# Moving steps between the turns of a fused attention and expert kernel

## The chip, the cores and the metric

One NeuronCore of a Trainium2 chip runs the whole computation. The metric is the device time of one execution in microseconds (us), for which a lower number is better. The kernel before takes 1458.46 us as the median of three runs (1452.64 to 1461.51). Beside these there is one profiled execution, from which every duration below is read.

## The reference

The input `x` has 8 batches of 512 tokens of 256 numbers, all float32. First comes attention with a convolution in the middle of it; then a second attention with a mixture of experts.

```python
# layer 1, on layernorm(x); 16 heads of 16, causal
q, k, v = split(x @ Wqkv.T + b)
ctx = attention(q, k, v)
q2  = conv1d(ctx, conv_w, width 3, padding 1) + conv_b    # over the tokens
x   = x + attention(q2, k, v) @ out_w.T + out_b
# layer 2, on layernorm(x)
h   = x + attention(rope(rmsnorm(x) @ wq), rope(rmsnorm(x) @ wk), rmsnorm(x) @ wv) @ wo
xf  = rmsnorm(h)
probs = softmax(xf @ w_router); the two largest of 8, scaled to a sum of 1
y   = h + sum over experts e of combine[e] * ((silu(xf @ wg[e]) * (xf @ wu[e])) @ wd[e])
```

In layer 2, `x` in the first line and in the sum `h` is that layer's normed input, as in the code; the outer residual is added to the whole. Every batch thus needs three attentions, and every token two of eight experts of width 704.

## The kernel before, in words

**Pairs and turns.** The batches go in four pairs, of which one batch is lane 0 (`one` in the plan) and the other lane 1 (`two`). Six attentions of a pair follow each other: `attention1` of lane 0 and of lane 1, `attention2` of both, `attention3` of both. An attention is a generator of nine steps. A step multiplies queries and keys into scores in PSUM (L1212, TensorE), takes the exponential of 1,024 columns twice (L1219, ScalarE) and masks the diagonal blocks (L1227, GpSimd). Its value products (L1142, TensorE) are not issued at once: they are put in the list `behind` and issued later by `catch_up`. A **turn** is two steps, so a pair takes 27 turns, and 108 turns make up the first 60% of the span.

**What else a turn holds.** The order on TensorE, VectorE, ScalarE and GpSimd is written out by hand: an engine executes what the program issues for it in that order. Between the steps stands all the other work of the pair, as units that the table of `plan` calls gives to a turn: `plan(t + 4, before1, "transpose3", 1)` means that in the fifth turn of this pair the method `transpose3(1)` of the previous pair's lane 1 is called. `before0` and `before1` are the batches of the pair before, `one` and `two` those of this pair, `next0` and `next1` those of the pair after. Units in `units` are called at the end of the turn, those in `first_units` and `small_units` between its two steps. Some work is delayed further: `follow(n, f, where)` calls `f` n turns later at "mid" (between the steps), "late" (after the second step, ahead of the turn's units) or "end" (after the units).

**The units that matter here.**
- `stats` and `normed` (L1305, L1320) are the first layer norm, on VectorE with a power on GpSimd (L1315); `transpose` (L1292, TensorE) turns the result, and VectorE or ScalarE copies it out of PSUM (L1296). `fetch_next` loads a batch from SP's queue.
- `q`, `k` and `values` are the projections (L1052, L1070 on TensorE). They are read out of PSUM at L1359 (VectorE) or L1357 (ScalarE), at L1342 (ScalarE) and at L1088 (VectorE, into the tile `va`).
- `normalise` (L1152) ends half an attention: ScalarE copies the sums (L1159), SP moves rows (L1167, L1168), and `finish` on VectorE takes reciprocals and products (L1172, L1173). In `attention1` the step `differences` follows (L1396 to L1399, the tiles `terms`), from which `conv` multiplies its quarters (L1408) and combines them (L1417 on ScalarE; L1422, L1426 on VectorE).
- `k2` and `q2` project and rotate (L1502 to L1508), and `values2` (L1534) projects the values of the third attention; its parameter `soon` decides whether VectorE or ScalarE copies into `va` (L1084).
- `h` (L1541) is the output projection: TensorE (L1041), an addition on VectorE (L1547), one on GpSimd (L1548), and squares on ScalarE that are written back into the same PSUM bank (L1550). `rms` (L1555) stores the batch and scales its rows (L1557, L1558, L1561).
- `transpose3` (L1565) turns the rows; the copy out of PSUM is VectorE's (L1298) with `soon` and ScalarE's (L1302) without. `logits` (L1568), `route` (L1583; some 25 tiny VectorE operations and one exponential, L1597) and `slots` (L1616; two small products, L1626 and L1627, and 16 tiny VectorE operations) choose the experts. Then GpSimd sends the rows to their places in DRAM, one transfer a step (L1650).

**Banks.** All units share two PSUM banks (`mm_tile`, L991), which they take in turn: a unit's product waits until the last but one has been read. The scores have two tiles of their own.

**Experts.** After the turns come 24 tiles of 384 tokens (`expert_tile`, L734). The first of them begins in the last turns: a generator whose first part turns the rows (L742, L745), whose second fetches sums, and whose next six are the hidden products (L764) with their activation (L778).

Of the kernel before, what the change touches and what calls it, by code (L numbers as in the profile page):

```python
# [19 lines left out]
B, S, D = 8, 512, 256  # L20
# [603 lines left out]
def fast_path(  # L624
# [29 lines left out]
    TURNS = 3 * STEPS  # L654
# [193 lines left out]
    with ExitStack() as att:  # L848
# [266 lines left out]
        def follow(turns, f, where):  # L1115
            due[where].append([turns, f])
# [6 lines left out]

        masked = []

        def attention(qT, kT, v, to, then=None, soon=False):

# [22 lines left out]
            def normalise(ch):  # L1152


                k = next(n_sums)
                cs = [big.tile([P, S], F32, tag=f"cs{i}", name=f"cs{i}") for i in range(2)]
                r = big.tile([P, S], F32, tag="r", name="r")
                for i in range(2):
                    nc.scalar.activation(  # L1159
                        cs[i], av[i], AF.Copy, accum_out=total[:, i, k : k + 1]  # L1160
                    )

                def part(t, i):
                    return t.rearrange("(f i) n -> i f n", i=2)[i]

                for i in range(2):
                    nc.sync.dma_start(part(r, i), part(cs[i], 1 - i))  # L1167
                nc.sync.dma_start(part(cs[1], 0), part(cs[0], 0))  # L1168

                def finish(n0):  # L1170
                    half = slice(n0, n0 + S // 2)
                    nc.vector.reciprocal(r[:, half], r[:, half])  # L1172
                    nc.vector.tensor_tensor(to[:, ch, half], cs[1][:, half], r[:, half], ALU.mult)  # L1173

                def check():
                    nc.scalar.activation(cs[0], r, AF.Copy, accum_out=rtotal[:, k : k + 1])

                where = ("mid", "late" if soon else "end")[ch]
                for n0 in range(0, S, S // 2):
                    follow(1 - ch, lambda n0=n0: finish(n0), where)  # L1180
                if then is not None:
                    follow(1 - ch, lambda: then(ch), where)
                follow(3 - 2 * ch, check, "late")
# [5 lines left out]
            mid = NB // 2  # L1189
# [65 lines left out]
        class Batch:  # L1255
# [108 lines left out]
            def attention1(self):  # L1364

                cx = self.cx = self.context_tile("cx")
                nc.gpsimd.memset(cx[:, :, 0:1], 0.0)
                nc.gpsimd.memset(cx[:, :, S + 1 : S + 2], 0.0)
                self.terms = {}
                return attention(  # L1370
                    self.qT, self.kT, self.v, cx[:, :, 1 : S + 1], self.differences, self.lane == 0
                )

# [295 lines left out]
        batches = [Batch(b) for b in range(B)]  # L1671
        units = collections.defaultdict(list)
# [3 lines left out]
        busy = set()  # L1676
# [5 lines left out]
        def plan(turn, t, what, *several, among=units):  # L1682
            if t is not None:
                if among is units and what not in NO_MATMULS:
                    busy.add(turn)
                for args in several or [()]:
                    args = args if isinstance(args, tuple) else (args,)
                    among[turn].append(unit(t, what, *args))
# [4 lines left out]
        for p in range(B // 2 + 1):  # L1693

            before0, before1, one, two, next0, next1 = (batch(2 * p + i) for i in range(-2, 4))
            if one is None:
                next0 = next1 = None
            t = p * TURNS
            plan(t, before0, "transpose3", (0, True), (1, True))
            plan(t, two, "q", 0)  # L1700
            plan(t, before0, "logits")
            plan(t + 1, two, "values", 0)
            plan(t + 1, before0, "route")
            plan(t + 1, before1, "normed2", 2, 3)
            plan(t + 1, next0, "stats")
            plan(t + 2, before1, "h", 0, 1)
            plan(t + 2, before0, "slots")
            plan(t + 2, before1, "rms")
            plan(t + 3, two, "q", 1, among=first_units)
            plan(t + 3, two, "k", 1)  # L1710
            plan(t + 3, next0, "fetch_next")
            plan(t + 3, next0, "normed")
            plan(t + 4, before1, "transpose3", (0, True))
            plan(t + 4, two, "values", 1)
            plan(t + 4, before1, "transpose3", 1)
            plan(t + 5, next0, "transpose", (0, True), (1, True), among=first_units)
            plan(t + 5, next0, "q", (0, True))
            plan(t + 6, before1, "logits")
            plan(t + 6, one, "conv", (0, 0))
            plan(t + 7, before1, "route")  # L1720
            plan(t + 7, one, "conv", (0, 1), (1, 0))
            plan(t + 8, one, "conv", (1, 1))
            plan(t + 9, next0, "k", 0)
            plan(t + 10, next0, "values", 0)
            plan(t + 10, before1, "slots")
            plan(t + 11, next0, "values", 1)
            for c in range(NC):
                plan(t + 10 + c, one, "bias", c)
                plan(t + 14 + c, two, "bias", c)
            plan(t + 12, two, "conv", (0, 0), among=first_units)  # L1730
            plan(t + 12, two, "conv", (0, 1))
            plan(t + 13, next0, "k", 1)
            plan(t + 14, two, "conv", (1, 0), among=first_units)
            plan(t + 14, two, "conv", (1, 1))
            plan(t + 15, one, "x1", 0, 1)
            plan(t + 16, next0, "q", 1)
            plan(t + 16, one, "transpose2", 0, 1)
            plan(t + 16, one, "k2", 0)
            plan(t + 16, one, "q2", 0)
            plan(t + 17, one, "q2", 1)  # L1740
            plan(t + 17, one, "k2", 1)
            plan(t + 18, one, "values2", 0, 1)
            plan(t + 19, two, "x1", 0, among=first_units)
            plan(t + 19, two, "x1", 1)
            plan(t + 20, one, "normed2", 0, 1, among=small_units)
            plan(t + 20, two, "transpose2", 0, 1)
            plan(t + 20, two, "k2", 0)
            plan(t + 21, two, "q2", (0, True), among=first_units)
            plan(t + 21, two, "k2", 1)
            plan(t + 20, next1, "stats")  # L1750
            plan(t + 21, next1, "fetch_next")
            plan(t + 21, next1, "normed")
            plan(t + 22, one, "normed2", 2, 3, among=small_units)
            plan(t + 23, two, "values2", (1, True), among=first_units)
            if next1 is not None:
                plan(t + 22, two, "q2", (1, False, False))
                plan(t + 23, two, "values2", (0, True))
                plan(t + 24, one, "h", 0)
                plan(t + 24, next1, "transpose", (0, True), (1, True))
                plan(t + 25, one, "h", 1)  # L1760
                plan(t + 25, one, "rms")
                plan(t + 26, two, "normed2", 0, 1, among=small_units)
                plan(t + 26, next1, "k", 0)
            else:
                plan(t + 22, two, "values2", 0)
                plan(t + 22, two, "q2", (1, False, False))
                plan(t + 24, one, "h", 0, 1)
                plan(t + 24, one, "rms")
                plan(t + 25, one, "transpose3", 0, 1)
                plan(t + 25, two, "normed2", 0, 1)  # L1770
                plan(t + 26, two, "normed2", 2, 3, among=small_units)
                plan(t + 26, one, "logits")
                plan(t + 26, one, "route")


        n_turns = B // 2 * TURNS
# [7 lines left out]
        one, two, later = batches[:3]  # L1784
# [32 lines left out]
        with tc.manual_schedule(  # L1817
# [3 lines left out]

            for _ in range(2):
                ps = mm_tile()
                for i in range(12):
                    nc.tensor.transpose(ps[:, i % NC * P : (i % NC + 1) * P], ident, ident)
            one, two = batches[:2]
            one.stats()
# [55 lines left out]
            first = {}  # L1883
# [4 lines left out]
                first["tile"] = expert_tile(first["weights"], rows, room)  # L1888

            units[n_turns - 4].append(first_tile_starts)  # L1890
            for n, parts_of in ((n_turns - 1, 4),):
                for _ in range(parts_of):
                    units[n].append(lambda: next(first["tile"]))
            steps = all_steps()
            for n in range(n_turns):
                behind_this = next(steps)

                rest = None if n in busy else max(1, len(behind) - 1)

                if n % TURNS in (6, 15, 24) and n in busy:  # L1900
                    rest = 2
                catch_up(rest)
                before_this = len(behind)
# [29 lines left out]
            t = batches[B - 1]  # L1933
# [103 lines left out]
```

## Time and profile before

| | |
|---|---|
| median of three runs | 1458.46 us (1452.64 to 1461.51) |
| the profiled execution | 1454.27 us |
| its span, first to last instruction | 1452.3 us |
| TensorE busy (products / weight loads) | 1384.3 / 893.9 us |
| VectorE, ScalarE, GpSimd busy | 744.0, 719.3, 580.2 us |
| mean granted TensorE clock | 0.985 |
| score and value products (L1212, L1142), busy | 282.9 and 224.0 us |
| expert products (L764, L788), busy | 347.0 and 190.9 us |
| first score exponential of turn 0, of turn 107 | 20.0 and 867.5 us |

How to read it: a busy TensorE need not be at its peak, since ends of products are modelled, but its idle time is read directly. A wait is put down to the instruction that came last. A granted clock below 1 means that products ran slower in that stretch.

### The profile page before, as it was taken

Reading aid. Unit: us, or ns where it says so; the run is one execution under the profiler, and the core shown is the slowest. Engines: PE = TensorE matmul, PEld = TensorE weight load, DVE = VectorE, ACT = ScalarE, POOL = GpSimd, SP = SyncE. Lnnn points to the kernel's source line nnn. Section 1 sums busy time; section 2 is a strip of 40 time slices with the busy share of each in tenths; the row PEclk is TensorE's granted clock in tenths of the full one; section 3 lists DMA queues with packets and bytes.
Section 4 is the critical chain, followed back from the end, with each engine's and each line's share of the span. In section 5 each row is a group of like instructions: output and inputs, shape, how many; then the busy total and the mean of one; then the engine's idle time right before and its main releaser. Section 6 shows DMA issues by size and latency. Waiting matters only on the chain. (4 is left out here: it accounts for less than half of the span.)

```text
span 1452.3 us, 32154 instructions
## 1 busy us (share of the span) xinstructions
PE 1384.3 (95%) x13466; PEld 893.9 (62%) x13466; DVE 744.0 (51%) x1467; ACT 719.3 (50%) x1164; POOL 580.2 (40%) x621
## 2 busy tenths in 40 slices
PE   8999989899989899989999998999999999999995
PEld 5566555566555566555565565666767667677673
DVE  4745886765886775885666865322222222222221
ACT  4677767577777676767676782311111111111110
POOL 3334333536433546433646345433233332332322
PEclk9999999999999999999999999999999999999998
DMA  5122122201001201011212022323131323232200
GB/s 147 58 80 87 63 78 75 75 31 61 16 24 52 93 31 57 16 43 38 88 58 81 24 78 83 113 83 117 42 110 47 105 64 98 60 107 86 84 20 16
DMA packets 62841, 97.61 MB, mean 67 GB/s; under 512 B 13516, under 2 KB 39064, under 8 KB 62688
## 3 DMA queue, kind: packets, MB, share of 16 engines
q1 hardware_dynamic: 52608, 69.74, 14.9%
q0 software_dynamic: 10080, 25.74, 5.3%
q8 instruction: 107, 1.75, 0.5%
q14 instruction: 46, 0.38, 0.1%
HBM read 46.06 MB, written 32.61 MB: 54 GB/s over the span
## 5 line engine op out<-in xcount | busy, mean ns | idle before, releaser
L1219 ACT ACTIVATE pr<-sc 128x1024 f32<-128x1024 f32 x432 | 418.8, 1023 | 169.2 <-PE sc L1212 168.2
L1227 POOL TENSOR_TENSOR pr<-pr,seen 128x512 f32<-128x512 f32 (+1 forms) x216 | 257.1, 1191 | 415.4 <-ACT pr L1219 407.1
L764 PE MATMUL pgu<-xgT,gu 128*128 128x384 f32 x1056 | 347.0, 488 | 1.6 <-DVE hT L779 1.6
L764 PEld LDWEIGHTS pgu<-xgT,gu 128*128 128x128 f32 x1056 | 200.7, 191 | 137.1 <-DVE hT L779 2.2
L778 ACT ACTIVATE sg<-pgu 128x384 f32<-128x384 f32 x120 | 58.8, 490 | 414.7 <-PE pgu L764 414.7
L1142 PE MATMUL av<-pr,va 64*32 64x448 f32 (+7 forms) x6144 | 224.0, 416 | 5.3 <-DVE va L1084 5.3
L779 DVE TENSOR_TENSOR hT<-sg,pgu 128x384 f32<-128x384 f32 x120 | 66.4, 554 | 247.0 <-ACT sg L778 247.0
L788 PE MATMUL po<-dn,hT 128*128 128x256 f32 x864 | 190.9, 379 | 1.6 <-POOL hT L759 1.6
L1212 PE MATMUL sc<-qT,kT 32*128 32x512 f32 (+7 forms) x2048 | 189.3, 440 | 2.9 <-ACT pr L1219 2.7
L805 POOL DMA_INDIRECT out_dram<-so_far,xg x72 | 72.4, 1006 | 288.8 <-DVE so_far L795 220.7
L1142 PEld LDWEIGHTS av<-pr,va 64*32 64x32 f32 x6144 | 113.7, 108 | 113.7 <-issue 84.4
L1172 DVE RECIPROCAL r<-r 128x256 f32<-128x256 f32 x96 | 167.5, 1745 | 27.2 <-DMA r<-cs 27.0
L788 PEld LDWEIGHTS po<-dn,hT 128*128 128x128 f32 x864 | 162.4, 190 | 23.6 <-POOL hT L759 2.0
L1212 PEld LDWEIGHTS sc<-qT,kT 32*128 32x128 f32 x2048 | 114.8, 186 | 75.6 <-issue 29.3
L795 DVE SCALAR_TENSOR_TENSOR so_far<-po,xg,so_far 128x256 f32<-128x256 f32 x72 | 34.8, 484 | 150.1 <-PE po L788 150.1
L750 POOL DMA_INDIRECT so_far<-out_dram,xg x72 | 74.0, 1028 | 53.7 <-issue 51.9
L1212 PE MATMUL sc<-q2T,kT 32*128 32x64 f32 (+7 forms) x1024 | 93.6, 434 | 0.8 <-ACT pr L1219 0.6
L1650 POOL DMA_INDIRECT xtab<-rows,slot x64 | 65.0, 1016 | 39.6 <-DVE pick L1639 23.5
L1212 PEld LDWEIGHTS sc<-q2T,kT 32*128 32x128 f32 x1024 | 58.1, 184 | 32.7 <-issue 14.6
L1408 PE MATMUL mm<-terms,conv_sb 128*128 128x256 f32 x256 | 63.5, 391 | 3.7 <-DVE terms L1397 3.7
L1052 PE MATMUL mm<-xT,wqkv_sb 128*128 128x512 f32 x128 | 64.3, 630 | 1.5 <-DVE xmT L1298 1.2
L1052 PE MATMUL mm<-xaT,wqkv_sb 128*128 128x512 f32 x128 | 61.3, 612 | 2.0 <-DVE xaT L1298 2.0
(178 smaller groups left out, 1355.3 us busy)
## 6 DMA issues: line engine op xcount, KB each, us to landing
r<-cs SPq DMA_DIRECT2D x96, 128.0 KB, 2.0
xtab<-pad SPq DMA_DIRECT2D x24, 397.5 KB, 3.5
xg<-xtab SPq DMA_DIRECT2D x24, 397.5 KB, 3.1
gu<-in_wg_dram SPq DMA_DIRECT2D x18, 352.0 KB, 3.2
cs<-cs SPq DMA_DIRECT2D x48, 128.0 KB, 1.9
dn<-in_wd_dram SPq DMA_DIRECT2D x9, 640.0 KB, 4.7
gu<-in_wu_dram SPq DMA_DIRECT2D x18, 320.0 KB, 4.3
out_dram<-x SPq DMA_DIRECT2D x9, 512.0 KB, 3.0
```

What stands on the lines that cost most here:

```text
L750: nc.gpsimd.indirect_dma_start(out=so_far[:, s, :], out_offset=None, in_=out, in_offset=token_of(xg, s), bounds_check=B * S - 1, oob_is_er ...
L764: nc.tensor.matmul(ps, gu[d][:, n0 : n0 + P], xgT[:, d, :], start=(d == 0), stop=(d == DC - 1),)
L779: nc.vector.tensor_mul(hT[k], sg, pu)
L788: nc.tensor.matmul(po, hT[k][:, s * P : (s + 1) * P], dn[:, k, :], start=(k == 0), stop=(k == NK - 1),)
L805: nc.gpsimd.indirect_dma_start(out=out, out_offset=token_of(xg, s), in_=so_far[:, s, :], in_offset=None, bounds_check=B * S - 1, oob_is_er ...
L1052: nc.tensor.matmul(ps, w[:, d, n0 : n0 + P], srcT[:, d, :S], start=(d == 0), stop=(d == DC - 1),)
L1142: nc.tensor.matmul(av[i][g * HP : (g + 1) * HP, j * KB :], v[rows, j, ch * G + g, :], pr[rows, g, at : at + n], start=(j == 0), stop=(j == ...
L1172: nc.vector.reciprocal(r[:, half], r[:, half])
L1212: nc.tensor.matmul(sc[:, g - g0, at : at + S - j * KB], kT[r0 : r0 + HP, ch, j], qT[r0 : r0 + HP, ch, j * KB : S], start=True, stop=True,)
L1219: nc.scalar.activation(pr[:, g0 : g0 + 2], sc, AF.Exp, scale=SCALE)
L1227: nc.gpsimd.tensor_tensor(diag, diag, seen.unsqueeze(1).unsqueeze(1).to_broadcast([P, G, len(parts), KB]), ALU.mult,).ins
L1650: nc.gpsimd.indirect_dma_start(out=xtab, out_offset=bass.IndirectOffsetOnAxis(ap=slot[:, c, k : k + 1], axis=0), in_=rows[:, c, :], in_off ...
```

## The change

The units are moved, and some copies out of PSUM change their engine:
- `attention` loses the parameter `soon`. In `attention1` of lane 0 the second `finish` and `differences` came at "late"; they now come at "end".
- `values2(0)` of lane 1 at t+23 and `transpose3(0)` of the previous lane 1 at t+4 lose their `True`, so ScalarE copies in place of VectorE.
- `next1.transpose` goes from t+24 to t+25.
- `next0.stats` goes from t+1 to t, and `slots` goes ahead of `h` in t+2.
- The quarters of lane 0's `conv` go from t+6, t+7 (two) and t+8 to t+7 (two, ahead of `route`), t+8 and t+9. `next0.values(0)` goes from t+10 to t+6, and `next0.k(0)` from t+9 to t+10.
- In the last pair `route` goes from the head of the last turn's expert work to a place behind three parts of the first expert tile.
- The number of transposes of the identity at the start, whose results nobody reads, goes from 2 × 12 to 2 × 17.
- In the last turns `catch_up` is no longer held to two entries (turn 96 is the one concerned).

```diff
...
         masked = []
-        def attention(qT, kT, v, to, then=None, soon=False):
+        def attention(qT, kT, v, to, then=None):
...
                 def check():
                     nc.scalar.activation(cs[0], r, AF.Copy, accum_out=rtotal[:, k : k + 1])
-                where = ("mid", "late" if soon else "end")[ch]
+                where = ("mid", "end")[ch]
                 for n0 in range(0, S, S // 2):
                     follow(1 - ch, lambda n0=n0: finish(n0), where)
                 if then is not None:
...
                 nc.gpsimd.memset(cx[:, :, 0:1], 0.0)
                 nc.gpsimd.memset(cx[:, :, S + 1 : S + 2], 0.0)
                 self.terms = {}
-                return attention(
-                    self.qT, self.kT, self.v, cx[:, :, 1 : S + 1], self.differences, self.lane == 0
-                )
+                return attention(self.qT, self.kT, self.v, cx[:, :, 1 : S + 1], self.differences)
...
             plan(t, before0, "transpose3", (0, True), (1, True))
             plan(t, two, "q", 0)
             plan(t, before0, "logits")
+            plan(t, next0, "stats")
             plan(t + 1, two, "values", 0)
             plan(t + 1, before0, "route")
             plan(t + 1, before1, "normed2", 2, 3)
-            plan(t + 1, next0, "stats")
+            plan(t + 2, before0, "slots")
             plan(t + 2, before1, "h", 0, 1)
-            plan(t + 2, before0, "slots")
             plan(t + 2, before1, "rms")
             plan(t + 3, two, "q", 1, among=first_units)
             plan(t + 3, two, "k", 1)
             plan(t + 3, next0, "fetch_next")
             plan(t + 3, next0, "normed")
-            plan(t + 4, before1, "transpose3", (0, True))
+            plan(t + 4, before1, "transpose3", 0)
             plan(t + 4, two, "values", 1)
             plan(t + 4, before1, "transpose3", 1)
             plan(t + 5, next0, "transpose", (0, True), (1, True), among=first_units)
             plan(t + 5, next0, "q", (0, True))
             plan(t + 6, before1, "logits")
-            plan(t + 6, one, "conv", (0, 0))
+            plan(t + 6, next0, "values", 0)
+            plan(t + 7, one, "conv", (0, 0), (0, 1))
             plan(t + 7, before1, "route")
-            plan(t + 7, one, "conv", (0, 1), (1, 0))
-            plan(t + 8, one, "conv", (1, 1))
-            plan(t + 9, next0, "k", 0)
-            plan(t + 10, next0, "values", 0)
+            plan(t + 8, one, "conv", (1, 0))
+            plan(t + 9, one, "conv", (1, 1))
+            plan(t + 10, next0, "k", 0)
             plan(t + 10, before1, "slots")
             plan(t + 11, next0, "values", 1)
             for c in range(NC):
...
             plan(t + 23, two, "values2", (1, True), among=first_units)
             if next1 is not None:
                 plan(t + 22, two, "q2", (1, False, False))
-                plan(t + 23, two, "values2", (0, True))
+                plan(t + 23, two, "values2", 0)
                 plan(t + 24, one, "h", 0)
-                plan(t + 24, next1, "transpose", (0, True), (1, True))
+                plan(t + 25, next1, "transpose", (0, True), (1, True))
                 plan(t + 25, one, "h", 1)
                 plan(t + 25, one, "rms")
                 plan(t + 26, two, "normed2", 0, 1, among=small_units)
...
                 plan(t + 25, two, "normed2", 0, 1)
                 plan(t + 26, two, "normed2", 2, 3, among=small_units)
                 plan(t + 26, one, "logits")
-                plan(t + 26, one, "route")
         n_turns = B // 2 * TURNS
...
             for _ in range(2):
                 ps = mm_tile()
-                for i in range(12):
+                for i in range(17):
                     nc.tensor.transpose(ps[:, i % NC * P : (i % NC + 1) * P], ident, ident)
             one, two = batches[:2]
             one.stats()
...
                 first["tile"] = expert_tile(first["weights"], rows, room)
             units[n_turns - 4].append(first_tile_starts)
-            for n, parts_of in ((n_turns - 1, 4),):
-                for _ in range(parts_of):
-                    units[n].append(lambda: next(first["tile"]))
+            for part in range(4):
+                if part == 3:
+                    plan(n_turns - 1, batches[B - 2], "route")
+                units[n_turns - 1].append(lambda: next(first["tile"]))
             steps = all_steps()
             for n in range(n_turns):
                 behind_this = next(steps)
                 rest = None if n in busy else max(1, len(behind) - 1)
-                if n % TURNS in (6, 15, 24) and n in busy:
+                if n % TURNS in (6, 15, 24) and n in busy and n + TURNS // 2 < n_turns:
                     rest = 2
                 catch_up(rest)
                 before_this = len(behind)
```

## The prediction

> **What bounds the kernel now.** First the page: TensorE (PE) is busy for 95% of the span, no other engine for more than 51%, and all of them wait for one another through TensorE's products. What can be won is therefore the time in which TensorE stands still, 1452.3 − 1384.3 = 68 us, and the time in which its clock is halved: a mean clock of 0.985 over the span is 22 us of lost clock, of which some 7 us lie behind the last product. The shares of busy time:
>
> ```profile
> PE 1384.3 (95%) x13466; PEld 893.9 (62%) x13466; DVE 744.0 (51%) x1467; ACT 719.3 (50%) x1164; POOL 580.2 (40%) x621
> ```
>
> Next, for whom TensorE waits (total, times, longest, in us). The first four lines and the sixth are results in PSUM that VectorE (DVE) or ScalarE (ACT) has not yet read, or tiles that they have not yet written:
>
> ```profile
> PE mm L1292 <- DVE xmT L1298: 8.6, 2, 4.4
> PE mm L1292 <- ACT mm L1550: 5.6, 3, 1.9
> PE av L1142 <- DVE va L1084: 5.3, 3, 1.8
> PE mm L1408 <- DVE terms L1397: 3.7, 4, 2.7
> ...
> PE mm L1587 <- DVE t L1581: 3.0, 1, 3.0
> ...
> PE mm L1626 <- ACT mm L1550: 1.8, 2, 1.1
> ```
>
> Third, the clock around two of them, by stretch (length, busy time of PE, PEld, DVE, ACT, POOL, then PEclk). In the stretch with the wait TensorE is busy for about half; in the next it is granted half the clock:
>
> ```profile
> 202.70:206.10 3.40, 1.78 (x26) 1.20 (x20) 3.33 (x4) 2.35 (x3) 1.42 (x1) 1.00 0.20 68
> 206.10:209.60 3.50, 3.34 (x40) 1.61 (x44) 3.35 (x5) 1.40 (x3) 1.28 (x1) 0.51 0.29 89
> 271.00:274.40 3.40, 0.72 (x14) 0.47 (x10) 3.24 (x6) 0.26 (x1) 1.84 (x2) 1.00 0.11 40
> 274.40:281.20 6.80, 5.24 (x53) 2.82 (x54) 2.79 (x6) 2.63 (x4) 0.00 (x0) 0.50 0.01 2
> ```
>
> So a wait of 1.8 us can cost 3.5. Last, why VectorE is late, in its timeline. Before the read of `va` it works off a rotation (L1505 to L1508):
>
> ```profile
> 203.76 1.64 DVE L1508 TENSOR_TENSOR qT<-t,t 128x512 f32<-128x512 f32 x1
> 205.43 1.41 DVE L1084 COPY va<-mm 64x512 f32<-64x512 f32 x2
> 206.87 1.75 DVE L1172 RECIPROCAL r<-r 128x256 f32<-128x256 f32 x1
> ```
>
> **What the skill says.** The Trainium skill, "TensorE: Matmul & The Clock Gate", section "What's actually happening", has the clock halved by an idle window of 3413 ns and restored by a busy one, with windows that run on freely. The trace agrees: its half-clock stretches are 3.4 or 6.8 us, and the same 1.78 us wait at 425.3, across a boundary, halves nothing. "PSUM — Partial Sum Buffer", "Engine vs sequencer instructions": ScalarE's and VectorE's queues are strictly first in, first out; so a moved step delays all behind it, as above. "SBUF — State Buffer", "Who interferes with whom": some VectorE operations wait for GpSimd's use of a shared port. The trace has L1561 at 335 to 2305 ns for one shape. "ScalarE: Activation LUTs", "What ACT_TABLE_LOAD costs": 1283 ns for a load and 1380 more for a drain; the trace shows loads of 1283 ns.
>
> **The change part by part.** All against the profiled execution's 1454.3 us (span 1452.3 and 2.0 around it). t is a pair's first turn.
>
> *Idle products.* 24 take 5.38 us and end at 8.05; the first real transposes wait until 9.79, and the clock is halved from 11.6 to 15.0. Ten more at 0.224 end at 10.3, at the 0.136 of a full-clock transpose (8 in 1.09) at 9.4: a cost of 0 to 0.5. If the half-clock stretch goes, 1.7 is won. I take −1.5 (−1.7 to +0.5).
>
> *`values2(0)` by ScalarE at t+23; the next batch's transposes at t+25 instead of t+24 (three pairs).* Each pair loses 1.78 (L1142 for `va`) and 1.88 (the second transpose at L1292, whose PSUM bank ScalarE squares into at L1550). The product ends at 203.16, ScalarE's exponentials at 203.29; two copies at 0.63 end near 204.6, and TensorE arrives at 204.49: 0.1 to 0.2 remain. The exponentials behind the copies start 0.3 late, with a score tile to spare. VectorE is freed of 1.4, so the first half of `c` stands at 205.4 + 1.75 + 0.43 = 207.6, and `h(0)` comes at 207.7, just behind it. One turn later the transposes' copies fall into an idle VectorE (3.2 busy of 10 us); `h(1)` needs the first one's bank, 0.2. At t+25 ScalarE's checks, squares and exponentials follow closely: 0.2. Won: 3 × (3.66 − 0.6) = 9.2. The half-clock stretches at 206, 216, 643 and 653 give 4 × 1.7 = 6.8, so −16.0 (−18 to −6).
>
> *`transpose3(0)` by ScalarE at t+4 (pairs 1 and 2; in pair 3 nothing waited).* VectorE reaches its copy only at 275.16, behind two reciprocals and four `terms`. ScalarE is free at 271.3, copies in 0.70, and TensorE, done at 271.72, waits 0.3. Won: 4.24 + 4.40 − 0.6 = 8.0. The half-clock stretches are 6.8 (5.24 busy, 2.6 lost) and 3.4 (1.7): 4.3. What is late next is VectorE's `va` (L1088) in the bank that the transposes of `xn` need. It would end at 276.6 and TensorE arrive at 275; the reciprocals start about 1 us sooner, since `rows` (L1561) no longer stand behind `slots`. I take no wait and keep 1.7 in the range: −12.3 (−14 to −8).
>
> *`stats` at t, `slots` before `h` at t+2.* `stats` puts 2.3 us on VectorE ahead of two reciprocals, so the `route` behind them comes 0.9 late; ScalarE's `prob` (L1597) is 0.9 late, and with it the exponentials behind it: TensorE's wait at 249.8 (0.81) grows to 1.7. `slots` takes 16 tiny products first. Their 4.0 us on VectorE (8 at 0.2, then 0.34, 1.11 and six at 0.2) now precede L1547, on which squares, exponentials and the next `q(1)` wait in turn. Worked through: L1547 at 257.1 (was 254.4), squares end at 259.8, exponentials start there (was 258.1), and `k(1)` starts at 262.3 (was 261.5). Two waits at L1626 (0.74, 1.08) are gone in that figure. Pair 3 had no such wait and loses 1.0. Queues passed: GpSimd's power (L1315) and the store that `rms` issues on SP move by about a microsecond, the load behind that store too; the row transfers still go out after the turn. +0.8 +0.8 +1.0, and 0.8 for a chance of a half-clock stretch: +3.4 (−1 to +8).
>
> *Convolution at t+7 to t+9, values at t+6, keys at t+10.* The wait for `terms` goes: 0.72 in pair 0, 0.15 in pair 1. `conv(0,0)`, `conv(0,1)` and `route` share two banks, and `route` then waits about 0.35 for L1422 in pairs 1 and 2. In pair 3 (2.69) nothing fills the turn, and ScalarE's exponentials and checks leave a new wait of 1.1 to 1.5 at L1212. Keys still follow the last quarter, whose `terms` lie in their tile. Sum −1.6 (−3.5 to +2).
>
> *`route` after three parts of the first expert tile.* The wait of 2.97 for L1581 stays in another dress: the second transposed half takes the bank of `logits`, which L1581 reads at 874.2. From 871.75 that is 2.4; the products start 0.9 earlier. Two more table loads fall between two activations, where ScalarE waits 2.1 us for products; uncovered they are 2 × 1.28, with the page's drain 2 × 2.66 as an estimate. −1.0 (−2.7 to +4).
>
> *`soon` and `rest`.* Between "late" and "end" of that turn stands no VectorE instruction, so the order there is the same: 0. One value product moves by half a turn in pair 3: 0 (±0.5).
>
> Sum: −1.5 − 16.0 − 12.3 + 3.4 − 1.6 − 1.0 = −29.0, so 1454.3 − 29.0 = 1425.3. The median shown is 4.2 above the profiled execution: 1429.5, rounded to **1430**.
>
> **Rivals.** *The next consumer waits instead* (0.13): `h(0)` has 0.1 us to spare behind `c`, and L1508 shows 1.64 where a free port gives 0.69. At 2 us in three turns, and 1.7 with a half-clock stretch of 1.7 in two, 12.8 come back: 1442. For it: VectorE is busy without a break from 262 to 277. Against: it idles 4.6 us right after.
> *The half-clock stretches stay* (0.10): windows run freely, and waits of 1.7 (turn 29) and 2.4 (first tile) remain. Seven stretches, 12 us: 1441.5. Against: a wait below 1.6 halved nothing.
> *Slower* (0.04): `stats` and `slots` on VectorE ahead of L1547 at t+2. If the shared port stretches them (L1637 took 1.11 instead of 0.19), L1547 is 6 us or more late, ScalarE holds the exponentials behind its squares, TensorE idles through whole windows in that turn and the two after it. It decides from 11 us per pair, when three outweigh the other steps' 32.4; at 6 us in each of three turns, 1454.3 − 32.4 + 54 + 4.2 = 1480.
>
> **The numbers.** This forecast 0.73, its own range 1419 to 1439. About 1% (14.6 us) is what a measurement of this kernel can tell from no change, so the bound is 1443.9. The two middle rivals lie below it with some six tenths of their chance: faster 0.86, same 0.11, slower 0.03. The range for 8 in 10 is 1418 to 1445: below, every step at its better end (−40.9, so 1417.6); above, both middle rivals in part.
>
> **What would show it.** Right: no `va L1084` by DVE, `xmT L1298` of 4 us or `mm L1550` among TensorE's waits; its idle time near 50 us; a clock of about 0.99. Wrong: waits at L1041 for `c`, at L1292 for `va L1088`, or at L1212 for exponentials in turns 29 and 30 (of 83 and 84 too) of more than 2 us, and half-clock stretches there.

## The result and the profile after

The kernel after takes **1441.05 us** (median of four executions, 1439.65 to 1443.23), the kernel before 1456.63 on the same chip (1452.64 to 1461.51). The ratio is 0.9893, with an interval of 0.9857 to 0.9928: 1.07% faster. The profiled execution of after takes 1439.65 us, its span is 1437.7 us and its mean clock 0.989. Profile against profile, after is 14.6 us shorter, where 29.0 were forecast.

TensorE stays as busy as it was (1384.3 and 1385.2 us, now with ten products more at the start); its gaps above 0.15 us went from 50.9 us to 35.1 us in all. So what was won is idle time. That the half-clock stretches up to the last product fell from 30.7 us to 17.1 in all did not make the busy time shorter; why is not shown. The first line below is the page's line of busy times, the others are TensorE's waits (total, times, longest, in us) from the view of waits of after. Its lines from about L1371 on are numbered two below those of before.

```profile
PE 1385.2 (96%) x13476; PEld 900.1 (63%) x13476; DVE 734.2 (51%) x1458; ACT 725.7 (50%) x1175; POOL 579.7 (40%) x621
...
PE sc L1212 <- ACT pr L1219: 7.1, 7, 2.3
PE mm L1292 <- DVE va L1088: 4.7, 2, 4.4
...
PE sc L1212 <- ACT kT L1519: 1.9, 3, 0.6
PE mm L1624 <- DVE both L1603: 1.7, 3, 0.9
...
PE mm L1041 <- DVE xT L1296: 1.0, 3, 0.3
```

The waits that the prediction set out to remove are gone: at L1292 for L1298 and for L1550, at L1142 for `va`, at L1408 for `terms`. New are three kinds: exponentials that come late (2.26 and 2.25 us in turns 29 and 56), the read of `va` (4.39 us), and small ones of 0.63 and 0.35 us behind `values2`. Two of the half-clock stretches of after, of 6.8 and 3.4 us, follow waits of the first two kinds (start and end, length, busy time of PE, PEld, DVE, ACT, POOL, PEclk, DMA share, GB/s):

```profile
242.40:245.80 3.40, 1.20 (x6) 0.59 (x8) 2.64 (x14) 3.02 (x5) 0.20 (x1) 1.00 0.02 5
245.80:252.60 6.80, 6.80 (x19) 4.43 (x17) 5.20 (x23) 2.05 (x2) 1.83 (x2) 0.50 0.00 0
484.70:488.10 3.40, 0.00 (x0) 0.00 (x0) 3.39 (x6) 1.27 (x5) 2.29 (x2) 1.00 0.26 97
488.10:491.60 3.50, 3.33 (x20) 2.50 (x24) 2.04 (x4) 0.00 (x0) 0.00 (x0) 0.51 0.15 57
```

From 484.7 to 488.1 TensorE does nothing at all, waiting for `va`. VectorE's timeline there (start, duration, operation, and in brackets how long it stood idle and for what) has the reason. SP's queue (the second view: start, duration, transfer) has the reason behind it:

```profile
471.95 2.51 DVE L1323 TENSOR_SCALAR xn<-x,mv,rstd 128x256 f32<-128x256 f32 x4
477.92 1.75 DVE L1172 RECIPROCAL r<-r 128x256 f32<-128x256 f32 x1 [3.46 <-DMA r<-cs]
481.73 0.43 DVE L1173 TENSOR_TENSOR cx<-cs,r 128x256 f32<-128x256 f32 x1 [2.05 <-DMA cs<-cs]
...
486.74 1.39 DVE L1088 TENSOR_TENSOR va<-mm,bv_sb 64x512 f32<-64x512 f32 x2
```
```profile
468.08 0.38 SPq L1266 DMA_DIRECT2D out_dram<-x  x1
471.10 0.38 SPq L679 DMA_DIRECT2D x<-in_x_dram  x1
471.58 1.11 SPq L1167 DMA_DIRECT2D r<-cs  x2
475.48 0.38 SPq L1266 DMA_DIRECT2D out_dram<-x  x1
477.91 0.47 SPq L1168 DMA_DIRECT2D cs<-cs  x1
```

VectorE is free at 474.5 and stands still for 3.46 us, because the rows for the reciprocal have not landed. They were issued at 471.58, behind the load of a batch that had itself waited for a store to land (468.08 to 471.10), and they arrive at 477.9, 6.3 us after their issue. The rows for `cx`, issued only then, cost another 2.05 us. The page of before gives 2.0 us as the median for one set of such rows. In before the same two sets took 6.0 us too (479.50 to 485.45, when L1168, which waits for them, goes out), but VectorE came to them only at 485.72, straight from the operation before, and waited for nothing:

```profile
479.50 1.11 SPq L1167 DMA_DIRECT2D r<-cs  x2
...
485.45 0.47 SPq L1168 DMA_DIRECT2D cs<-cs  x1
```
```profile
485.72 1.74 DVE L1172 RECIPROCAL r<-r 128x256 f32<-128x256 f32 x1
```

Where the 14.6 us came from is read from the start of each turn's first exponential, after minus before. A half-clock stretch counts in the turn that it falls in:

| stretch (turns) | forecast | profile |
|---|---|---|
| start to turn 0 (idle products) | −1.5 | −2.1 |
| `values2(0)` and transposes, three pairs (24–26, 51–53, 78–79) | −16.0 | −12.0 |
| `transpose3`, `stats`, `slots` (27–36, 53–64, 82–87) | −12.3 + 3.4 | +2.9 (−1.9, +2.4, +2.4) |
| the rest: convolution, drift, tail | −2.6 | −3.4 |

### The profile page after: what moved, and what is told of

Same layout as the page of the kernel before. It is cut to its first block, busy times and chain, and to the rows that moved or that the text cites. A ratio compares the mean times of both kernels' runs of the same rounds, so it can differ in the third digit from the quotient of the medians.

```text
span 1437.7 us, 32181 instructions
## 1 busy us (share of the span) xinstructions
PE 1385.2 (96%) x13476; PEld 900.1 (63%) x13476; DVE 734.2 (51%) x1458; ACT 725.7 (50%) x1175; POOL 579.7 (40%) x621
## 5 line engine op out<-in xcount | busy, mean ns | idle before, releaser
L1142 PE MATMUL av<-pr,va 64*32 64x512 f32 (+7 forms) x6144 | 218.9, 407 | 0.0
L1212 PE MATMUL sc<-qT,kT 32*128 32x320 f32 (+7 forms) x2048 | 192.4, 436 | 8.3 <-ACT pr L1219 6.2
L1172 DVE RECIPROCAL r<-r 128x256 f32<-128x256 f32 x96 | 167.5, 1744 | 20.5 <-DMA r<-cs 20.4
L1142 PEld LDWEIGHTS av<-pr,va 64*32 64x32 f32 x6144 | 113.4, 106 | 102.5 <-issue 73.7
L1212 PE MATMUL sc<-q2T,kT 32*128 32x512 f32 (+7 forms) x1024 | 95.0, 434 | 1.3 <-ACT pr L1219 0.9
L1648 POOL DMA_INDIRECT xtab<-rows,slot x64 | 64.6, 1009 | 32.1 <-DVE pick L1637 15.6
```

The source lines that it names most:

```text
L1142: nc.tensor.matmul(av[i][g * HP : (g + 1) * HP, j * KB :], v[rows, j, ch * G + g, :], pr[rows, g, at : at + n], start=(j == 0), stop=(j == ...
L1212: nc.tensor.matmul(sc[:, g - g0, at : at + S - j * KB], kT[r0 : r0 + HP, ch, j], qT[r0 : r0 + HP, ch, j * KB : S], start=True, stop=True,)
L1648: nc.gpsimd.indirect_dma_start(out=xtab, out_offset=bass.IndirectOffsetOnAxis(ap=slot[:, c, k : k + 1], axis=0), in_=rows[:, c, :], in_off ...
```

## The experiments

Theory A: half of the forecast gain is lost because `stats` and `slots`, ahead of the route and of the sum L1545 on VectorE, delay ScalarE's exponentials. Rival B: it is lost in VectorE's reads that wait for rows from SP's queue, so that the next consumer waits. Three chips were used: one for the first three experiments below and the load held back, one for `stats`, `slots` and the load's turn, one for the rest. So a ratio below is to the kernel before on the same chip; one thousandth is 1.45 us.

**`transpose3(0)` alone, in the kernel before.**

```diff
-            plan(t + 4, before1, "transpose3", (0, True))
+            plan(t + 4, before1, "transpose3", 0)
```

> The kernel before, with `transpose3(0)` at t+4 copied by ScalarE as the only edit. As predicted (the waits of 4.24 and 4.40 us at L1292 for L1298 and two half-clock stretches go): 8 to 12 us shorter, ratio about 0.993. Rival B (VectorE's `va`, L1088, for the transposes of `xn`, is late by about the same): the waits come back under that name, 2 us in pair 1 and 4.6 us in pair 2, with a half-clock stretch each, and the time is within 3 us of before.

1447.60 us (11 executions), ratio 0.9967 (0.9951 to 0.9983): 4.8 us faster, give or take 2.3, where 12.3 were forecast. In its view of waits the two of 4.24 and 4.40 us have become these:

```profile
PE mm L1292 <- DVE va L1088: 2.9, 2, 1.5
```

The next consumer waits, but for 2.9 us and not for 8.6. It is not the rows of B that it waits for: in both pairs VectorE goes from `xn` into the reciprocals without a pause, as in pair 2 here, and stands idle for at most 0.23 us up to `va`.

```profile
479.86 2.55 DVE L1323 TENSOR_SCALAR xn<-x,mv,rstd 128x256 f32<-128x256 f32 x4
482.34 1.74 DVE L1172 RECIPROCAL r<-r 128x256 f32<-128x256 f32 x1
```

What is late here is VectorE's own queue. By the starts of the turns the two pairs gain 4.4 and 3.5 us.

**`values2(0)` and the transposes alone, in the kernel before.**

```diff
-                plan(t + 23, two, "values2", (0, True))
+                plan(t + 23, two, "values2", 0)
                 plan(t + 24, one, "h", 0)
-                plan(t + 24, next1, "transpose", (0, True), (1, True))
+                plan(t + 25, next1, "transpose", (0, True), (1, True))
```

> The kernel before, with `values2(0)` at t+23 copied by ScalarE and `next1.transpose` at t+25 as the only edits. As predicted: 16 us shorter (9.2 of waits, 6.8 of half-clock), ratio about 0.989. As the starts of the turns in the kernel after have it: 12 us shorter, ratio about 0.992, with new waits of 0.63 us at L1212 for the split keys and 0.35 us at L1041 three times each. Theory A says nothing else: no wait above 1 us between turns 23 and 28.

1444.38 us (20 executions), ratio 0.9941 (0.9925 to 0.9957): 8.6 us faster. The starts of the turns give −4.9, −2.0 and −5.1, the same as in the kernel after, so this step works by itself. The waits of 11.0 us went, and these came:

```profile
PE sc L1212 <- ACT kT L1521: 1.9, 3, 0.6
...
PE mm L1041 <- DVE xT L1296: 1.0, 3, 0.3
```

The four half-clock stretches of 3.4 us went from these turns. But two came, at 248 and 739 us. Of those that both kernels have, the one at the start and the one in pair 2 (493 us in before, 483 here) grew from 3.4 to 6.8 us, and the one in pair 1 (274, here 272) shrank from 6.8 to 3.4. In all, the half clock up to the last product is 3.4 us shorter, which is 1.7 us of lost clock and not 6.8: the profile's mean clock is 0.986 against 0.985. In the timed executions the gain is larger, 0.9871 as a mean of 20 against 0.9835 of 34.

**The kernel after without `transpose3(0)`.**

```diff
-            plan(t + 4, before1, "transpose3", 0)
+            plan(t + 4, before1, "transpose3", (0, True))
```

> The kernel after, with `transpose3(0)` at t+4 back on VectorE. If the step is worth what the starts of the turns say (6 us in pair 1, 0 in pair 2): 6 us longer than the kernel after, ratio about 0.9935. As predicted (12): ratio about 0.998. Rival B (the wait is the same whoever copies, because VectorE's reciprocals wait for their rows): waits at L1292 of 2 to 4 us for L1298 in place of `va`, within 3 us of the kernel after.

1445.68 us, ratio 0.9949 (0.9930 to 0.9968), 8 us longer than after by the ratios, give or take 6. TensorE's wait stands under its old name again, and is nearly as long as in before (8.6):

```profile
PE mm L1292 <- DVE xmT L1298: 7.7, 2, 5.2
```

So the early `stats` and `slots` do not shorten that wait by themselves. In pair 2 (5.2 us) VectorE again stands still for the rows, 3.44 us ahead of L1172, as B says. But B's "within 3 us" is not what the times show. The step is worth some 8 us in this company where it gave 4.8 alone; with these uncertainties the two are not told apart.

**`stats` back, `slots` back, both back.**

```diff
-            plan(t, next0, "stats")
...
+            plan(t + 1, next0, "stats")
...
-            plan(t + 2, before0, "slots")
             plan(t + 2, before1, "h", 0, 1)
+            plan(t + 2, before0, "slots")
```

> The kernel after, with `stats` of the next batch back at t+1; `slots` stay ahead of `h`. Theory A (half of the forecast gain is eaten because `stats` and `slots`, ahead of the route and of the sum L1547 on VectorE, delay ScalarE's exponentials): the wait at L1212 for L1219 in turns 29, 57/58 falls from 2.26 and 2.25 us to about 0.8, the half-clock stretch of 6.8 us at 245.8 and that of 3.4 us at 460.8 go, and the profiled execution is 5 to 6 us shorter, about 1434. Rival B (the loss sits in VectorE's reads that wait for rows from SP's queue): within 1 us of the kernel after, 1440.

> The kernel after, with `slots` back behind `h` at t+2; `stats` stay at t. Theory A: the two waits of 0.7 to 1.1 us at L1624 for the squares of L1548 come back (about 1.8 in all), the sums L1545 start about 4 us sooner behind the third step, so turns 30 and 31 give back 2 to 3 us per pair less: 2 to 4 us shorter than the kernel after, about 1437. The waits of 2.25 us in turns 29 and 58 stay. Rival B: within 1 us, and the wait of 4.39 us at L1292 for `va` of L1088 in pair 2 unchanged.

> The kernel after, with `stats` at t+1 and `slots` behind `h`, as before the change; every other part of the change stays. Theory A: about 8 to 10 us shorter than the kernel after, 1430 to 1432, with turns 28 to 31 and 57 to 58 no later against the kernel before than turn 28. Theory A with B: the reciprocals then come later and VectorE's `va` (L1088) becomes the wait in both pairs (2 to 4 us each): 1434 to 1438. B alone: 1440.

`stats` back: 1437.12 us, ratio 0.9893 (0.9860 to 0.9927), the same as after. Its waits of 2.25 us fell to 0.80, as expected, but TensorE then waited 1.88 us twice at L1041, because `h` needs the bank that `slots` reads at L1628, and again 4.25 us for `va`. `slots` back: 1430.26 us, 0.9840 (0.9804 to 0.9875), more than either theory expected. It is the one kernel of the three in which the wait for `va` in pair 2 is short, 0.60 us, since its rows landed 4.7 us after their issue and VectorE came to them just then. Both back: 1433.13 us, 0.9870 (0.9838 to 0.9901); no late exponentials, but

```profile
PE mm L1292 <- DVE va L1088: 6.6, 2, 4.6
```

Theory A alone would have that at 1430 to 1432 with nothing late next; A with a late next consumer fits. The rows are only part of that: VectorE stands still for them for 1.89 us in pair 2, and not at all in pair 1. By the ratios `stats` and `slots` together cost 3.3 us (0.9893 − 0.9870), not 10; the intervals overlap. The kernel of the next experiment, timed on this chip, can stand for after: against it `stats` back wins 0.1 us, `slots` back 7.0 and both back 4.1, and in the last two cases every execution is faster than all four of that kernel. So the parts do not add up. What goes with the place of `slots` is the wait for the rows of pair 2: in the five kernels with `slots` ahead of `h` and no hold, VectorE stands still for 3.4 to 3.6 us ahead of L1172, in the five with `slots` behind it for less than 0.1.

**The load at another turn.**

```diff
-            plan(t + 3, next0, "fetch_next")
...
             plan(t + 6, before1, "logits")
+            plan(t + 6, next0, "fetch_next")
```

> The kernel after, with the load of the next batch (L679, `fetch_next`) at the end of t+6 instead of t+3, so that the rows of L1167 are not issued on SP's queue right behind it. Rival B as the cause in pair 2: L1167's rows land 2 to 2.5 us after issue instead of 6.3 (471.6 to 477.9), VectorE's `va` (L1088) ends 3 to 4 us sooner, the wait of 4.39 us at L1292 and the half-clock stretch at 488.1 go: 4 to 6 us shorter, about 1434.5. If it isn't the load ahead in the queue (another transfer, the stores of L1266, GpSimd's row transfers): same landing, within 1 us of 1440.

1437.24 us, ratio 0.9900 (0.9869 to 0.9932). The edit did nothing to what it was meant for. SP's order is not written out by the plan: the load stands directly behind the store that frees its buffer, at t+3 and at t+6 alike, and the rows again took 6.2 us (471.92 to 478.15). In the first pair one batch is loaded a second time. Read as the kernel after once more (with that one load too many), it gives that kernel's ratio a second time, and shows how the wait for `va` varies: 2.78 us here, 4.39 there.

**The load held back.**

```diff
-    def load_x(b):
+    def load_x(b, held=False):
         if b < B:
             xs[b] = keep.tile([P, NC, D], F32, tag="x", name="x", bufs=4)
+            if held:
+                nc.gpsimd.memset(xs[b][:, 0, 0:2], 0.0)
...
-                load_x(self.b + 1)
+                load_x(self.b + 1, self.b % 2 == 0 and self.b > 2)
...
-            plan(t + 3, next0, "fetch_next")
+            plan(t + 3, next0 if p == 0 else None, "fetch_next")
...
+            plan(t + 6, next0 if p else None, "fetch_next")
```

> The kernel after, with the load of batches 5 and 7 (L679) held back to the end of t+6 by a write of two of its elements per row on GpSimd, so that it stands behind two more sets of L1167 on SP's queue, and neither the load nor its wait for the store's landing is ahead of the rows. Rival B as the cause of the 4.39 us in pair 2: the rows land at most 3 us after their issue (6.3 in the kernel after), the reciprocal starts 3 us sooner, the wait at L1292 for `va` of L1088 falls below 1 us and the half-clock stretch at 488 goes: 4 to 6 us shorter than the kernel after, ratio to before about 0.986 where 0.9895 is that of the kernel after. If the rows are slow for another reason (GpSimd's row transfers): landing and wait stay, within 1 us of the kernel after.

In pairs 1 and 2 the load can't be issued here before GpSimd's write of t+6 (line numbers are two above those of after). SP's and VectorE's timelines:

```profile
466.64 0.38 SPq L1268 DMA_DIRECT2D out_dram<-x  x1
468.87 1.10 SPq L1169 DMA_DIRECT2D r<-cs  x2
471.41 0.47 SPq L1170 DMA_DIRECT2D cs<-cs  x1
```
```profile
470.51 2.52 DVE L1325 TENSOR_SCALAR xn<-x,mv,rstd 128x256 f32<-128x256 f32 x4
472.95 1.74 DVE L1174 RECIPROCAL r<-r 128x256 f32<-128x256 f32 x1
474.78 0.43 DVE L1175 TENSOR_TENSOR cx<-cs,r 128x256 f32<-128x256 f32 x1
```

The rows land 2.5 us after their issue instead of 6.3, VectorE goes from `xn` to the reciprocal without a break, `va` is read at 479.8 instead of 486.7 (1.5 us of that had been gained before turn 58), and TensorE has no wait at L1294 for it above 0.15 us. The mechanism of B is shown for pair 2: the load, and its wait for the store, ahead of the rows. Counted from the start of `xn`, the rows land 5.1 us sooner; 1.3 of that lie before their issue and 3.8 in their landing. In the profile pair 2 gains 5.7 us more than in after (−3.2 against +2.4, turns 53 to 64). Pair 1 gains 1.4 more (−3.3 against −1.9, turns 27 to 36), but 1.2 of that stand in turn 29, before the turn of the load, where a half-clock stretch is 3.4 us long and not 6.8. In the timed executions less shows: 1435.43 us, ratio 0.9888 (0.9859 to 0.9916), within the interval of after. What this wait is worth on average is left open; it differs from one execution to the next.

**The two causes together.**

> The kernel after, with `slots` back behind `h` and the load of batches 5 and 7 held back to t+6. Theory A (the order of `stats` and `slots` on VectorE) and rival B (rows behind the load on SP's queue) as separate causes: the loss of 2 to 3 us per pair at `slots` and the wait for `va` are both gone, only the 2.25 us at L1212 in turns 29 and 56 and their half-clock stretches stay; ratio about 0.982, 1 to 3 us shorter than with `slots` moved back alone (0.984). If B was only a follow-up of A: same as with `slots` moved back alone.

> The kernel after, with `stats` at t+1, `slots` behind `h`, and the load held back to t+6. A and B separate: with both moved back the waits for `va` were 2.0 and 4.63 us and two half-clock stretches; of these the part that VectorE spends in waits for L1168's rows (1.9 us in pair 2) goes, the rest (VectorE's own work behind `stats`) stays: waits of about 2 and 2.5 us, ratio 0.984 to 0.986. If the load is the whole cause of those waits: below 0.5 us each, ratio about 0.982.

`slots` back with the load held: 1435.75 us, ratio 0.9870 (0.9824 to 0.9915), a miss: 0.982 was expected. The wait for `va` was only 0.60 us without the hold, so there was little to win. Up to turn 107 its profile is 0.7 us ahead of that kernel's; then half-clock stretches at 888 and 936 us, and a wait of 2.4 us ahead of the second, all in the experts' part that no edit touches, more than take it back. Both back with the load held: 1430.13 us, 0.9837 (0.9796 to 0.9878), with these waits for `va`, 1.34 and 1.05 us, instead of 2.00 and 4.63:

```profile
PE mm L1294 <- DVE va L1090: 2.4, 2, 1.3
```

Below 0.5 us each was expected if the load were the whole cause, about 2 and 2.5 if VectorE's own work were the rest. It lies between: VectorE now goes from `xn` to `va` without a pause, so what stays is its own queue. Up to the last product its profile has no half-clock stretch at all. With the load held the starts of the turns give `stats` and `slots` a cost of 3.5 us in three pairs, by the change in the same turns: −4.4, −4.0 and +0.7 here, −3.3, −3.2 and +2.4 with the load held alone.

**`stats` at the head of its turn, with `slots` back and the load held.**

```diff
             t = p * TURNS
+            plan(t, next0, "stats")
             plan(t, before0, "transpose3", (0, True), (1, True))
             plan(t, two, "q", 0)
             plan(t, before0, "logits")
-            plan(t, next0, "stats")
```

> The kernel with `slots` behind `h` and the load held back, and `stats` at the head of the units of turn t, ahead of `transpose3`, instead of at their end. Theory A: VectorE has 1.4 us to spare at either side of `transpose3`'s copies there, so the reciprocals of t+1 are no longer behind `stats`; the wait at L1212 in turns 29 and 56 falls from 2.25 to about 0.8 and their half-clock stretches go, against a new wait of 0.5 to 1.5 us at L1052 for L1298: ratio about 0.979 to 0.981. If `stats` there wait for the landing of the batch, TensorE waits 2 us or more for L1298 in turn t: ratio 0.983 or above.

1428.80 us, ratio 0.9827 (0.9786 to 0.9867), where 0.979 to 0.981 was expected. It is the lowest ratio of all, but its interval overlaps those of `slots` back and of both back. On the same chip it is 7.0 us below the kernel with `stats` at the end of the turn (1435.75, `slots` back with the load held), and each of its executions is faster than all four of that one. The two kinds of TensorE's waits that the edit touches:

```profile
PE sc L1214 <- ACT pr L1221: 4.3, 7, 0.8
...
PE mm L1054 <- DVE xmT L1300: 2.6, 3, 1.1
```

The late exponentials are at 0.8 again, though the half-clock stretch near 247 stays, where it was expected to go. The price is two waits of 1.08 us for VectorE's copies, which now stand behind `stats`. Without this edit VectorE was idle there for 1.57 us ahead of these copies and for 1.42 behind them:

```profile
228.27 0.42 DVE L1037 BATCH_NORM_STATS2 st<-x 128x6 f32<-128x256 f32 x1
...
230.61 1.40 DVE L1300 TENSOR_SCALAR xmT<-mm,g_sb 128x512 f32<-128x512 f32 x2
233.43 0.75 DVE L1361 TENSOR_SCALAR qT<-mm,bqk_sb 128x512 f32<-128x512 f32 x1 [1.42 <-PE mm L1054]
```

**The convolution, values and keys at their old turns.**

```diff
-            plan(t + 6, next0, "values", 0)
-            plan(t + 7, one, "conv", (0, 0), (0, 1))
+            plan(t + 6, one, "conv", (0, 0))
             plan(t + 7, before1, "route")
-            plan(t + 8, one, "conv", (1, 0))
-            plan(t + 9, one, "conv", (1, 1))
-            plan(t + 10, next0, "k", 0)
+            plan(t + 7, one, "conv", (0, 1), (1, 0))
+            plan(t + 8, one, "conv", (1, 1))
+            plan(t + 9, next0, "k", 0)
+            plan(t + 10, next0, "values", 0)
```

> The kernel after, with the convolution's quarters, the values and the keys of the next batch back at their turns of before (t+6, t+7, t+8; t+10; t+9). As predicted: the waits at L1406 for `terms` come back (0.7 us in pair 0, 2.7 us in pair 3), 1.6 us longer than the kernel after, ratio about 0.9905; by the starts of the turns up to 3 us longer. Lines of cause A and B are untouched: waits of 2.25 us at L1212 and of 4.4 us at L1292 as in the kernel after.

1443.40 us, ratio 0.9911 (0.9883 to 0.9940), 2.6 us longer than after by the ratios, with an interval that doesn't exclude zero. The wait for `terms` came back with 0.72 us in pair 0 and with only 0.75 in pair 3, where 2.7 was expected; what else of the change shortened it there is not shown. The other waits are those of after (2.25 twice, 4.70).

## Why the prediction was right or wrong

Sign and range held: faster, and 1441 lies between 1418 and 1445. The number, 1430, was 11 us too low, and 1441 lies outside the 1419 to 1439 of the forecast's own mechanism. Its two largest terms came out at about half by themselves. Both middle rivals had forecast that size, 1442 and 1441.5, and each holds a part.

- *Idle products*, −1.5: the stretch at half clock at the start went, and the first exponential of turn 0 comes 2.1 us sooner. Over all profiles it lies 1.7 to 2.3 us ahead of before with 17 products, and between 1.2 ahead and 0.2 behind with 12. Right.
- *`values2(0)` and the transposes*, −16.0: alone 8.6 us. The nine microseconds of waits were right in mechanism and, in the profile, nearly in size: 11.0 gone and 2.9 new. Most of the new (0.63 each) is a wait for the keys that ScalarE splits at L1519, which the sum did not have: TensorE, which no longer waits for `va`, comes to them too soon. The other term, "the half-clock stretches at 206, 216, 643 and 653 give 4 × 1.7", treated a stretch as belonging to the wait before it. In the profile 1.7 us of lost clock went, not 6.8, because other waits filled other windows, as the rival on half-clock stretches has it. In the timed executions the mean clock rose by 3.6 thousandths; at the 1.2 us for each that the executions of before show (last section), that is an estimate of 4.4 us. Then 4.2 would be left for the waits. So the two terms together were 7.4 us too high, and how that divides between them is open.
- *`transpose3(0)`*, −12.3: alone 4.8 us. "It would end at 276.6 and TensorE arrive at 275" is a wait of 1.6 for `va`, and with `slots` in their old place it came, 1.4 and 1.5 us. The step that was to remove it, "the reciprocals start about 1 us sooner … I take no wait", needs `slots` ahead of `h`. In pair 1 of the kernel after it held: the reciprocals start 2.2 us sooner, counted from their turn, and the wait is 0.3. In pair 2 it failed. VectorE's queue was free even 4.0 us sooner (474.46, against 485.72 less the 7.24 us that the turn itself came sooner), but the reciprocals also need rows from SP's queue, and the prediction did not look at these. In before VectorE came to L1172 1.7 us after the rows in pair 1 and 0.27 us after them in pair 2, so in pair 2 there was next to nothing to start sooner. A wait of 4.4 us for `va` took the place of the old one; with both others back it was 4.6, next to 2.0 in pair 1. The rival "the next consumer waits instead" had the right mechanism and not this place: it named `h` behind `c`.
- *`stats` at t, `slots` before `h`*, +3.4: 3.3 us by the ratios and 4.1 on one chip without the hold, 3.5 by the starts of the turns with it, and 7.4 by the ratios with it, give or take 7. The size was about right as far as this tells. Theory A with its 8 to 10 us fell without the hold; the times with it do not rule that out. The wait in turn 29 grew to 2.26 where 1.7 was estimated. Of the queues passed, the line "the load behind that store too" was written down but given no price; that load is what the rows stand behind.
- *Convolution*, −1.6: 2.6 by the ratios, not told apart from 1.6. The feared new wait in pair 3 was 0.59.
- *`route` after three parts*, −1.0: the tail gained 2.6 in the profile. In place of the residual 2.4 stand waits of 0.60 for `xgT` and 0.94 for `both`, and the half-clock stretch at 875 went. It was not tried by itself, and some of it can be chance: with `transpose3(0)` alone, which leaves `route` where it was, the wait of 2.97 at L1587 was 1.1.

The sum in medians, with the tail and the start from the profile: −8.6 − 4.8 − 2.6 − 2.1 − 2.6 + 3.4 = −17.3, against −15.6 measured; with the 8 us that `transpose3(0)` gave in company it is −20.5. With several us of uncertainty in it, the sum shows only that the parts are of the right size together.

The slow rival, `stats` and `slots` ahead of L1547, had the right place with the wrong weight. It needed 11 us per pair; the cost was one to two and a half in each. The rival on half-clock stretches had "a wait below 1.6 halved nothing" against it; in the kernel after a stretch follows a wait of 0.81 us (last section).

## What to carry to other kernels

When a stall is taken away, list everything that the next consumer needs, its transfers too, and look in the timeline at how close behind their landing it runs now: 0.27 us of slack hides a queue that will be the next wait. An operation on a busy in-order engine does least harm where that engine stands idle on both sides, as with `stats` at the head of its turn here. A half-clock stretch was not a fixed price of the wait in front of it, so price the clock as an average over many executions, and not stretch by stretch from one profile.

## What was unexpected in the hardware

- One and the same program, before, took 1449.1 to 1462.1 us in 34 executions on one chip, while its mean granted clock ran from 0.987 to 0.978. The two go together (correlation −0.94), at 1.2 us for each thousandth. The mean clock was 0.9835 there; with both moved back and the load held it was 0.9952 in four executions on another chip, where before had 0.9829.
- The same wait can halve the clock or not. All fourteen profiles have a wait of 0.80 to 0.82 us at the score product in turn 83. In five, after among them, a half-clock stretch follows within 3 us; in nine none does. That a window falls on a wait by chance agrees with the free-running windows of the Trainium skill, "TensorE: Matmul & The Clock Gate", "What's actually happening". Nor need TensorE stand still for a whole window: in after it was busy for 2.21 of the 3.4 us before such a stretch (columns as above).

```profile
672.50:675.90 3.40, 2.21 (x15) 0.69 (x9) 3.02 (x12) 3.02 (x4) 1.30 (x1) 1.00 0.00 0
675.90:679.30 3.40, 3.40 (x10) 2.93 (x11) 2.75 (x18) 0.68 (x1) 0.72 (x1) 0.50 0.00 0
```

- A small transfer shared the fate of a large one beside it. The two sets of rows that landed 2.5 us after their issue with the load held took 4.9 in pair 1 and 6.3 in pair 2 of the kernel after, beside the load of a batch, while the 16 DMA engines were almost full (DMA share 0.93 in this stretch of after):

```profile
474.00:478.00 4.00, 4.00 (x104) 2.29 (x104) 0.55 (x2) 2.12 (x3) 2.89 (x4) 1.00 0.93 325
```

- A load that waited for a store's landing (3.0 us from 468.08 to 471.10, the page of before's median for the landing of such a store) held up SP's queue: the rows behind it went out at 471.58.
